# Two TensorE steps of a scan are given a due time in the scheduler that orders the queues

## The chip, the core and the metric

The kernel runs on one core of a Trainium2 chip. The metric is device time in microseconds (us), the median of several runs. Engines are named as in the profile: PE is TensorE's matmul (PEld its weight load), DVE is VectorE, ACT is ScalarE, POOL is GpSimd, SP is SyncE, which only issues transfers here.

## The reference, cut to what matters

Four images of 96 channels and 64 x 64 pixels pass through four layers. Layer 0 is a selective scan in four directions, layer 1 a deformable convolution, layer 2 a Fourier mixer with a quantised feed-forward part, layer 3 linear attention with another feed-forward part. Only the scan of layer 0 is touched:

```python
def step(h, inp):
    d_t, u_t, b_t, c_t = inp
    dA = jnp.exp(d_t[..., None] * A)
    h = dA * h + (d_t * u_t)[..., None] * b_t[:, :, None, :]
    y = jnp.einsum('bkdn,bkn->bkd', h, c_t)
    return (h, y)
h0 = jnp.zeros(u.shape[:3] + (A.shape[-1],), u.dtype)
_, ys = lax.scan(step, h0, (dl, ul, bl, cl))
```

There are 4 images, 4 directions, 192 channels, 16 states for each channel and 4096 positions.

## The kernel before

**Units.** The scan is cut into 1536 units: 4 images x 4 directions x 4 stretches of 1024 positions x 3 groups of 64 channels x 8 sets of 8 channels. A unit has 8 channels times 16 states on the 128 partitions and 1024 positions along the free dimension. Eight units in a row form a block, which ends in one tile of sums, `py`. Each unit passes through these steps:

- `fetch` (L956): a transfer on ACT's queue brings the step widths into `da`, one of six buffers, five units ahead.
- `decay` (L1000): ACT turns `da` into exp(da * A).
- `inflow` (L1006), the **spreading product**: two matmuls copy the unit's 8 rows of delta times u over the 16 states, into `db` in PSUM. `db` has two buffers of 1024 float32 per partition, so the product of unit n+2 writes where the scan of unit n reads.
- `enter` (L1020): DVE multiplies `db` by B in place.
- `recur` (L1028): DVE runs the scan itself, from `da` and `db` into `hh`, one of six buffers.
- `weigh` (L1035, L1037): POOL keeps the last state and multiplies `hh` by C.
- `total` (L1056), the **state sum**: for a pair of units, four matmuls sum the 16 states into `py`. The first pair of a block (`u.i == 0`) opens `py`, in three directions of four with four more matmuls (L1051) that bring in an earlier direction or the skip term. There is one `py` tile, so opening it waits for the copy out of the block before.
- `settle` (L1067): ACT copies a finished `py` to `yb`; `store` (L1074) sends it out from SP's queue.

**The loop over units.** `scan` goes once through its loop for each unit n and emits, in this order, a few loads, `inflow(n+1)`, `decay(n+2)`, for odd n `total(n-5, n-4)`, `fetch(n+5)`, `recur(n)`, `weigh(n-2)` and, at the end of a block, `settle` and `store`. Then it yields, and other work is emitted until none fits: this is called the **fill** below.

**The fill.** Two streams supply it. One (`ends`) prepares the inputs of the scans of images 1 to 3 (convolution L750, `steps` L827 to L880) and then carries each image through layers 2 and 3, one image after another. The other (`middle`) takes the scanned images through the end of layer 0 (`behind`, L1120 to L1177) and through layer 1 (sampling L1369 to L1425). Both are generators; `pipe` runs several chains of steps side by side.

**The clock.** Each engine executes its instructions in the order in which they were emitted; `in_program_order` fixes that order. `Clock` decides it: it keeps for each engine an estimated end, `ends`, to which each emitted step adds its estimated cost. The costs here are 0.8 for a product, 1.22 for `enter`, 2.33 for a scan, 2.55 for `weigh`, 1.5 for a sum and 1.3 more where it opens `py`. A fill step is emitted only where `has_room` finds its inputs ready and its engines no further ahead of `now()` than `AHEAD` (3.0 us for PE, 3.0 DVE, 5.0 ACT, 7.0 POOL). `now()` is the end of DVE's queue or `due`, whichever is later, and `due` moves on by `PACE`, 4.5 us, with each unit. `self.scanned[1]` is the estimated end of the latest scan. One step of the scan is already left to the clock: `precede`, which `pipe` calls ahead of each fill step, emits `enter` of the next unit first when that fill step has DVE work and the product is estimated to be done by then.

A state sum makes itself wait, in the estimate, for three things:

```python
ready = max(u.weighed, v.weighed, self.settled if u.i == 0 else 0.0)
u.summed = v.summed = self.net.clock.add(PE, 1.5 + 1.3 * (u.i == 0), ready)
```

Of the kernel before, what the change touches and what calls it, by code (L numbers as in the profile page):

```python
# [1 line left out]

# [1 line left out]

# [191 lines left out]
PE, DVE, ACT, POOL = range(4)  # L196
# [10 lines left out]
class Clock:  # L207
# [4 lines left out]
    def __init__(self):  # L212
# [8 lines left out]

        self.enter, self.entered = None, 0.0

    def now(self):
        return max(self.ends[DVE], self.due) if self.own is None else self.own

# [15 lines left out]
    def precede(self, work):  # L242


        if self.enter and work[DVE] and self.own is None and self.entered + MARGIN <= self.ends[DVE]:
            self.enter()

    def add(self, engine, us, ready):
        self.ends[engine] = max(self.ends[engine], ready) + us
        return self.ends[engine]  # L250
# [99 lines left out]
class Net:  # L350
# [29 lines left out]
    def load(self, name, pool, tag=None):  # L380
        src = self.ins[name]
        t = pool.tile(list(src.shape), F32, name="w_" + name, tag=tag or "w_" + name)
        self.nc.sync.dma_start(t, src)
        return t
# [158 lines left out]
class Layer0:  # L543
# [340 lines left out]
    def scan(self):  # L884


        units = [
            Unit(b, k, step, g, i, q)
            for b in range(B)
            for k in ((1, 3, 0, 2) if b else (0, 1, 3, 2))  # L890
            for step in range(NT)
            for g in range(NG)
            for i in range(4)
            for q in range(2)
        ]
        ahead = 5
        loaded = 0
        clock = self.net.clock

        def at(m):  # L900
            return units[m] if 0 <= m < len(units) else None

        def made(u):
            return all(
                (u.b, u.k, both, 2 * u.j + h) in self.ready for both in (False, True) for h in range(2)
            )

        for n in range(len(units) + 7):
            for m in range(loaded, min(n + ahead + 1, len(units))):
                while not made(units[m]):  # L910
                    yield False
            if n == 0:
                while loaded < ahead:
                    self.fetch(units[loaded], units[loaded - 1] if loaded else None)
                    loaded += 1
                self.decay(at(0))
                self.decay(at(1))
                self.inflow(at(0))
                self.next = at(0)
                self.enter()  # L920

            for period, tick, load in ((24, 12, self.fetch_step), (8, 2, self.fetch_block)):
                u = at(n - n % period + period)
                if n % period == tick and u is not None and made(u):
                    load(u)
            for stage, m in ((self.inflow, n + 1), (self.decay, n + 2)):
                if at(m) is not None:
                    stage(at(m))
            if n % 2 == 1 and at(n - 5) is not None:
                self.total(at(n - 5), at(n - 4))  # L930
            if loaded < len(units):
                self.fetch(units[loaded], units[loaded - 1])
                loaded += 1
            if at(n) is not None:
                self.recur(at(n), at(n - 6).summed if n >= 6 else 0.0)
            if at(n - 2) is not None:
                self.weigh(at(n - 2))
            if n % 2 == 0 and at(n - 6) is not None and at(n - 6).i == 3:
                self.settle(at(n - 6))
            if n % 2 == 1 and at(n - 7) is not None and at(n - 7).i == 3:  # L940
                self.store(at(n - 7))
            clock.unit(self.scanned[1])
            self.next = at(n + 1)
            if self.next is not None:
                clock.enter, clock.entered = self.enter, self.next.spread
            yield True
            if clock.enter:
                self.enter()
# [913 lines left out]
```

## Time and profile before

| what | us |
|---|---|
| median of 3 runs | 8791.93 |
| lowest and highest | 8787.54, 8800.51 |
| the profiled execution's own time | 8796.72 |
| its span, first to last instruction | 8794.9 |
| scans: first product to last sum | 197 to 7511 of the span |
| after the last scan | 7511 to 8795 |

| engine | busy in the span | busy from 197 to 7511 us |
|---|---|---|
| PE | 6606.4 (75%) | 5441.07 |
| DVE | 6862.6 (78%) | 6252.56 |
| ACT | 4917.9 (56%) | 4427.94 |
| POOL | 5603.0 (64%) | 5224.41 |

The mean granted PE clock is 0.813. How to read it: the scan phase takes five sixths of the span, and the DVE has the most work in it; what follows it is the last image's way through the other layers and what was left over of the image before. The span is one execution, profiled; its own time is 4.8 us above the median.

### The profile page before, as it was taken

How to read it: one execution, taken by the hardware profiler on the slowest of the kernel's cores; microseconds unless marked ns; L12 is line 12 of the kernel's file. 1: busy time of each engine (PE TensorE's matmuls, PEld its weight loads, DVE VectorE, ACT ScalarE, POOL GpSimd, SP SyncE). 2: the span in 40 equal slices, each digit the busy share in tenths (PEclk: the TensorE clock that was granted, in tenths of full speed). 3: DMA queues.
4: the chain of work that ended last, by engine and by line, in shares of the span. 5: the costliest groups of instructions: out<-in, count | busy, mean ns of one | idle time of the engine just before them, and what ended most of it. 6: DMA issues, size and time to landing. Idle time of an engine off the chain costs nothing.

```text
span 8794.9 us, 96335 instructions
## 1 busy us (share of the span) xinstructions
PE 6606.4 (75%) x31960; PEld 2922.3 (33%) x31960; DVE 6862.6 (78%) x5155; ACT 4917.9 (56%) x9030; POOL 5603.0 (64%) x4291
## 2 busy tenths in 40 slices
PE   6665877679677776877677687777768887779697
PEld 2211221123232322321222354322325552367283
DVE  2799989989798988778899887788887878367414
ACT  4554566546577776655666765345676665322323
POOL 0565666666588887656688886566888776167000
PEclk8876887779788777887778788877888887888887
DMA  3577677877788888777788888766888787255110
GB/s 87 165 199 191 180 194 216 213 185 196 197 234 238 234 225 211 188 186 190 213 237 223 233 221 195 184 167 181 217 209 224 210 219 165 62 164 174 28 52 11
DMA packets 775990, 1608.41 MB, mean 183 GB/s; under 512 B 247809, under 2 KB 339357, under 8 KB 773382
## 3 DMA queue, kind: packets, MB, share of 16 engines
q10 hardware_dynamic: 244224, 843.17, 36.9%
q1 hardware_dynamic: 457542, 532.51, 22.4%
q0 software_dynamic: 73728, 226.57, 9.8%
q8 instruction: 257, 4.21, 0.2%
q14 instruction: 239, 1.96, 0.1%
HBM read 1345.62 MB, written 256.29 MB: 182 GB/s over the span
## 4 chain that ended last, share of the span: by engine, by line
PE 34%; DVE 27%; DMA 17%; ACT 8%; issue 7%; POOL 2%; SPq 2%; ACTq 1%; DVEq 0%; POOLq 0%
DVE hh L1028 13%; DVE db L1020 7%; DMA du<-du 4%; PE pc L750 4%; PE py L1056 4%; PE f L1496 3%; PE ps L1402 3%; DMA da<-de 3%; PE db L1006 3%; ACT g L1381 2%; DMA bc<-bcd 2%; PE pd L1418 2%; ACT da L1000 2%; PE h L1537 1%; POOL hh L1037 1%
## 5 line engine op out<-in xcount | busy, mean ns | idle before, releaser
L1037 POOL TENSOR_TENSOR hh<-hh,bc 128x1024 f32<-128x1024 f32 x1536 | 3661.5, 2386 | 385.4 <-DVE hh L1028 275.6
L1028 DVE TENSOR_TENSOR_SCAN hh<-da,st,db 128x1024 f32<-128x1024 f32 x1152 | 2700.8, 2344 | 183.4 <-PE py L1056 63.9
L1020 DVE TENSOR_TENSOR db<-db,bc 128x1024 f32<-128x1024 f32 x1536 | 1862.9, 1213 | 579.5 <-PE db L1006 577.9
L1000 ACT ACTIVATE da<-da,w_al 128x1024 f32<-128x1024 f32 x1536 | 1740.4, 1146 | 628.8 <-DMA da<-de 207.6
L1006 PE MATMUL db<-du,rep 96*128 96x512 bf16 x3072 | 1093.9, 444 | 899.2 <-DVE hh L1028 853.0
L1369 POOL DMA_INDIRECT g<-table,idx x1152 | 1213.2, 1053 | 366.5 <-issue 179.2
L1056 PE MATMUL py<-hh,w_fold 128*32 128x512 f32 x6144 | 1050.0, 757 | 7.5 <-issue 3.7
L1381 ACT ACTIVATE g<-g,wt 128x96 f32<-128x96 f32 x3456 | 963.8, 364 | 157.6 <-DVE hh L1028 52.4
L1028 DVE TENSOR_TENSOR_SCAN hh<-da,db 128x1024 f32<-128x1024 f32 x384 | 877.3, 2285 | 96.9 <-PE py L1056 43.7
L1006 PEld LDWEIGHTS <-rep 96*128 96x128 bf16 x3072 | 281.2, 106 | 1872.0 <-issue 1195.2
L1402 PE MATMUL ps<-w_ident,g 128*96 128x128 f32 x3744 | 694.4, 328 | 195.8 <-ACT g L1381 130.5
L838 POOL TENSOR_TENSOR lw<-lw,w 128x512 f32<-128x512 f32 x192 | 243.9, 1270 | 722.1 <-DVE w L836 651.0
L1402 PEld LDWEIGHTS ps<-w_ident,g 128*96 128x96 f32 x3744 | 495.7, 145 | 570.3 <-ACT g L1381 258.5
L1035 POOL COPY st<-hh 128x1 f32<-128x1 f32 x1152 | 231.4, 201 | 668.7 <-DVE hh L1028 625.0
L750 PE MATMUL pc<-pad,wc 96*128 96x512 f32 x1152 | 570.7, 629 | 12.2 <-DVE rl L840 3.7
L1410 ACT COPY st<-ps 96x384 f32<-96x384 f32 x384 | 179.7, 474 | 457.6 <-PE ps L1402 415.0
L869 PE MATMUL pr<-ex,w_ident 128*128 128x512 f32 x384 | 281.3, 823 | 152.6 <-DVE ex L859 83.8
L750 PEld LDWEIGHTS pc<-pad,wc 96*128 96x128 f32 x1152 | 220.8, 199 | 320.3 <-issue 284.7
L1056 PEld LDWEIGHTS py<-hh,w_fold 128*32 128x32 f32 x6144 | 154.6, 122 | 493.0 <-issue 367.5
L827 PE MATMUL pd<-xd,w_dtw 103*64 103x512 f32 (+1 forms) x512 | 249.1, 740 | 53.6 <-DVE rl L840 28.4
L1418 PE MATMUL pd<-st,wdc 96*128 96x256 f32 x1152 | 286.5, 396 | 3.6 <-ACT st L1410 1.8
L1505 ACT COPY d<-f 128x512 f32<-128x512 f32 x192 | 111.8, 583 | 305.3 <-PE f L1496 291.2
(252 smaller groups left out, 8829.0 us busy)
## 6 DMA issues: line engine op xcount, KB each, us to landing
da<-de ACTq DMA_DIRECT2D x1536, 512.0 KB
du<-du SPq DMA_DIRECT2D x512, 192.0 KB
bc<-bcd SPq DMA_DIRECT2D x128, 512.0 KB
du<-du SPq DMA_DIRECT2D x128, 384.0 KB
y<-yb SPq DMA_DIRECT2D x384, 128.0 KB
de<-rl SPq DMA_DIRECT2D x128, 256.0 KB
m<-in_dft SPq DMA_DIRECT2D x128, 256.0 KB
ad<-y ACTq DMA_DIRECT2D x192, 128.0 KB
```

What stands on the lines that cost most here:

```text
L750: nc.tensor.matmul(pp, lhsT=wc[:, q, g * 128 : (g + 1) * 128], rhs=pad[:, r0 + dy : r0 + dy + NR, dx : dx + W], start=(q == 0), stop=(q == 8),
L869: nc.tensor.matmul(pr, lhsT=net.ident, rhs=ex, start=True, stop=False)
L1000: self.net.nc.scalar.activation(u.da, u.da, AF.Exp, scale=self.al[:, a : a + 1])
L1006: self.net.nc.tensor.matmul(db[:, h, :], lhsT=self.rep[:96, u.s % 4, :], rhs=u.du[u.s // 4][:, h * CH : (h + 1) * CH], start=True, stop=True,)
L1020: self.net.nc.vector.tensor_mul(u.db, u.db, u.bc[:, 0, :])
L1028: nc.vector.tensor_tensor_scan(u.along(u.hh), u.along(u.da), u.along(u.db), first, ALU.mult, ALU.add)
L1037: self.net.nc.gpsimd.tensor_mul(u.hh, u.hh, u.bc[:, 1, :])
L1056: nc.tensor.matmul(py[p0 : p0 + 32], lhsT=self.fold[:, u.i, :], rhs=hc[:, h * CH : (h + 1) * CH], start=u.sums["add"] is None and u.i == 0 ...
L1369: nc.gpsimd.indirect_dma_start(out=g[:, k, :], out_offset=None, in_=self.tables[b % 2], in_offset=bass.IndirectOffsetOnAxis(ap=idx[:, n : ...
L1381: nc.scalar.activation(pixel, pixel, AF.Identity, scale=wt[:, n, c : c + 1])
L1402: nc.tensor.matmul(pt[:, k, :], lhsT=g[:, k, c * C : (c + 1) * C], rhs=net.ident, is_transpose=True, start=(c == 0), stop=(c == corners - 1),)
L1418: nc.tensor.matmul(po, lhsT=wdc[:, k, :], rhs=st[:, k, :], start=(k == 0), stop=(k == 8))
```

## The change

The product of unit n+2 and the sum of a pair are no longer emitted at the head of the next unit only. They are put into a list of the clock, `early`, each with the time from which it is due: the product from the estimated end of scan n, the sum from the estimated end of the later `weigh`. `precede`, which runs ahead of each fill step that `pipe` emits, now also emits every entry of that list that is due by PE's estimated end, if the fill step has PE work. What is still in the list at the next unit's head is emitted there, where both steps stood before.

```diff
@@ class Clock
+        self.early = []
...
         if self.enter and work[DVE] and self.own is None and self.entered + MARGIN <= self.ends[DVE]:
             self.enter()
+        if work[PE] and self.own is None:
+            for due in [e for e in self.early if e[0] <= self.ends[PE]]:
+                self.early.remove(due)
+                due[1]()
...
@@ def scan, head of a unit
-            for stage, m in ((self.inflow, n + 1), (self.decay, n + 2)):
-                if at(m) is not None:
-                    stage(at(m))
-            if n % 2 == 1 and at(n - 5) is not None:
-                self.total(at(n - 5), at(n - 4))
+            while clock.early:
+                clock.early.pop(0)[1]()
+            if n == 0:
+                self.inflow(at(1))
+            if at(n + 2) is not None:
+                self.decay(at(n + 2))
...
@@ def scan, ahead of the yield
+            if at(n + 2) is not None:
+                clock.early.append((self.scanned[1], partial(self.inflow, at(n + 2))))
+            if n % 2 == 0 and at(n - 4) is not None:
+                u, v = at(n - 4), at(n - 3)
+                clock.early.append((max(u.weighed, v.weighed), partial(self.total, u, v)))
             yield True
```

No instruction is added or removed, and no buffer changes. `self.settled`, the third thing that a sum waits for, is not in the due time of the list.

More of the change, by code (lines that the diff above doesn't have):

```diff
@@ L1 @@
 from contextlib import ExitStack
+from functools import partial
 import numpy as np
```

## The prediction

> **What bounds the kernel now.** I read the page's groups first, then busy time by stretch, the waits of DVE and PE, and a timeline of the worst wait.
>
> The groups give the scan's cost on DVE, one product (L1020) and one scan (L1028) for each of 1536 units:
>
> ```profile
> L1028 DVE TENSOR_TENSOR_SCAN hh<-da,st,db 128x1024 f32<-128x1024 f32 x1152 | 2700.8, 2344 | 183.4 <-PE py L1056 63.9
> L1020 DVE TENSOR_TENSOR db<-db,bc 128x1024 f32<-128x1024 f32 x1536 | 1862.9, 1213 | 579.5 <-PE db L1006 577.9
> ...
> L1006 PE MATMUL db<-du,rep 96*128 96x512 bf16 x3072 | 1093.9, 444 | 899.2 <-DVE hh L1028 853.0
> ...
> L1028 DVE TENSOR_TENSOR_SCAN hh<-da,db 128x1024 f32<-128x1024 f32 x384 | 877.3, 2285 | 96.9 <-PE py L1056 43.7
> ```
>
> A unit needs 1.21 + 2.34 = 3.55 us of DVE. Busy time by stretch, cut at the first product and the last sum, shows how far from that the scans are (columns: stretch, length, then busy us of PE, PEld, DVE, ACT, POOL, PE clock, DMA share, GB/s):
>
> ```profile
> 197.00:7511.00 7314.00, 5441.07 (x24486) 2174.39 (x24486) 6252.56 (x4219) 4427.94 (x8110) 5224.41 (x3960) 0.81 0.77 203
> 7511.00:8795.00 1284.00, 1035.79 (x7204) 696.64 (x7202) 577.28 (x875) 391.98 (x793) 369.56 (x316) 0.83 0.29 83
> ```
>
> 7314 / 1536 is 4.76 us a unit. DVE is busy for 6252.6: 5441 for the scan's own two steps and 812 for fill. It idles for 1061. The waits in the same stretch say on what, and what PE waits for in turn:
>
> ```profile
> DVE db L1020 <- PE db L1006: 577.9, 209, 31.2
> DVE hh L1028 <- PE py L1056: 107.6, 77, 17.7
> DVE w L836 <- ACT w L833: 43.3, 32, 7.3
> ...
> PE db L1006 <- DVE hh L1028: 853.0, 449, 15.9
> ```
>
> So 686 of 1061 idle us end with exactly the two steps that the change moves. DVE is the bound of this phase, but through the order of PE's queue, not through PE's capacity: PE idles for 7314 - 5441 = 1873 us, 853 of them at a product whose `db` buffer a scan still holds. The worst case, in the timeline:
>
> ```profile
> 5489.02 2.35 DVE L1028 TENSOR_TENSOR_SCAN hh<-da,st,db 128x1024 f32<-128x1024 f32 x1
> ...
> 5505.77 2.07 PE L1125 MATMUL pc<-ya,w_cen_a 128*128 128x512 f32 x2 [18.74 <-POOL ya L1120]
> ...
> 5513.00 0.83 PE L1006 MATMUL db<-du,rep 96*128 96x512 bf16 x2
> ...
> 5513.87 1.23 DVE L1020 TENSOR_TENSOR db<-db,bc 128x1024 f32<-128x1024 f32 x1 [22.49 <-PE db L1006]
> ```
>
> The product at 5513 could have run from 5487, when its buffer came free. It stands behind a fill matmul that waits 18.74 us for late data.
>
> The phase after the scans ends with the stream that takes images through layers 2 and 3 in turn: in the trace image 1 leaves at 7716, image 2 at 8309 and image 3 at 8787, while the sampling of image 3 is over at 8172. Fill that does not fit beside the scans therefore comes back at the end.
>
> **What the Trainium skill says.** "PSUM — Partial Sum Buffer", section Engine vs sequencer instructions, says that matmuls start and complete in program order and that the other three engines' queues are strict FIFO. The trace agrees: nothing passed L1125 for 18.74 us. So a moved step holds up all that is queued behind it. The same page, Specifications, gives 8 banks of 2 KiB (512 float32) per partition: `db` takes four, `py` one, the fill three, so the one-unit reach of `db` and the single `py` stay the limits. The trace shows both: products wait for scans, opening a sum waits for `yb`. "Perfetto Trace Analysis", Identifying the Most-Contended Engine, takes occupancy as a fair measure for VectorE and warns that it isn't for TensorE; I use PE's busy time only to split it into fill and scan.
>
> **The change, part by part.** It adds and removes no instruction. A moved product is two weight loads and two matmuls (0.6 us), a moved sum eight records of each (1.07 us), twice that where it opens `py` with L1051. Neither issues a transfer, and only PE's queue changes directly. The call itself costs nothing on the chip.
>
> *Where they go.* Read unit by unit from the trace, the product of n+2 starts 2.37 us after the end of scan n on average, over 2 us in 643 units of 1534 and over 3 us in 439. Meanwhile PE is busy for 2901 of these 3640 us. In those stretches PE's estimate runs ahead of the scan's, the entry is due at the first or second PE step of the fill, and the product jumps a unit's fill. Where PE is early, it stays where it was.
>
> *Gain at the product.* A product that is earlier by one place can let DVE run on by one unit at most, 3.55 us: the product after it is still behind the same fill. If every late product stood right behind the one before it, the waits would shrink by 540 us; each capped at 3.55 this is 356. About half the late ones should get it, since some entries come due only after the step that blocks, and part of the time saved only moves to the next wait: 0.5 x 356 = 178.
>
> *Gain at the sum.* The sum has been ready for long: it starts 11.5 us (median) after POOL's last product for it. It goes ahead of the fill as well, `hh` comes free sooner, and half of the 107.6 us goes: 54. Together 232.
>
> *Loss at `py`.* The first sum of each block, 192 of them, is due by `weigh` alone, but needs the copy `yb` (ACT, L1067), which was emitted just before in the same unit. It used to stand one unit later. The copy ends 2.31 us (median) after the product that would now stand ahead of it; counted from the end of scan n plus 0.6 us for the product, it is late by 251 us summed over the blocks. For that long PE stands still with fill, and sometimes the next product, behind it; the clock charges it too, so less fill is emitted. PE is 74% busy in the scans, so 251 x 0.74 = 186 us of PE work is lost to them. It returns at the end, where PE is busy for 1035.8 of 1284 us (81%): 186 / 0.81 = 230. The scans lose DVE fill in return: 812 us of it goes with about 3090 us of PE fill (5441 less 1094, 1050 and about 205 for L1051, whose first 768 of 1152 records take 136.7), 0.26, so 48 come off. Loss 182. Bounds: 0 if PE has nothing to do just then; 562 us of holding (copy against product, all blocks), so 0.74 / 0.81 x 562 less 108 = 405, if PE is always short.
>
> *Loss at the fill.* PE's fill of a unit now starts behind a product that waits for a scan, up to a unit later. DVE consumers stand in fixed places: of the 64 `d<-h` (L1545) within the scans a quarter started less than 1.4 us after their matmul, half less than 2.8. Some 400 DVE fill steps read PE's results directly; a quarter of them late by 1 us is 100. That is an estimate; the trace of before has no such order. Bounds: 0, as `enter` now comes ahead of DVE's fill and gives 1.21 us of cover, and 300.
>
> *At nothing:* `decay`, `fetch`, `weigh`, `recur` and the loads keep their order on ACT, POOL, DVE and SP. `enter` ahead of fill moves 1.21 us, it adds none; its cover is the product's earlier place.
>
> Sum against the profiled execution's 8796.7: -232 + 182 + 100 = +50, so 8847. That execution is 4.8 above the median of the runs: **8842**. What is late next: fill results on DVE, and the opening of `py`.
>
> **Rivals.**
> - *Faster (0.36).* The hold at `py` falls into PE's idle time, of which there are 1873 us. Then three quarters of the gains, 0.75 x (356 + 108) = 348, stand against 200 of losses: about 8645, from 8560 to 8770. For it: DVE waited little for fill before (43.3 us is the largest). Against: each wait taken from DVE makes PE the one that waits. It decides if the hold costs under 80 us.
> - *No difference (0.10).* The entries are seldom due, and are emitted at the unit's head as before: 8792. The 643 late products speak against it.
> - *Much slower (0.12, part of slower).* PE loses its reserve: the 1087 products that did not wait for a scan now wait 0.25 us each, 270 us with fill behind. By the conversion above this is 195 more: about 9035. The 853 us, 449 waits, speak for it; PE's 26% of slack against.
> - *The forecast (0.42):* 8800 to 8930 on its own.
>
> Below 0.2% (18 us) this kernel's measurement can't tell a change from none. **Chances:** faster 0.36, same 0.10, slower 0.54. The range runs from 8610 (a tenth below, in the faster case) to 8980 (a tenth above).
>
> **What would show it.** Right: L1020's wait for L1006 falls from 578 to about 400, L1056's hold on scans to 55; PE's wait for `yb` at L1051 (105 us in 36 cases) grows past 250; PE's wait for scans at L1006 rises above 853; the last sum comes before 7511 and the end phase is longer than 1284. Wrong: an end phase no longer than before with the scans shorter (the faster rival), DVE's new waits at L840, L836 and L1545 above 300 us (much slower), or a PE order that hardly differs.

## The result, and the profile after

| | before | after |
|---|---|---|
| median of the runs, us | 8789.74 (4 runs, 8776.73 to 8800.51) | 9018.36 (4 runs, 9008.85 to 9027.76) |
| ratio, 95% interval | | **1.0266** (1.0246 to 1.0285): slower |
| the profiled execution, span, mean granted PE clock | 8796.72, 8794.9, 0.813 | 9026.73, 9024.9, 0.816 |

Slower by 2.7%, 230 us between the spans. The direction was forecast, the size was not: 50 us, and a range that ended at 8980.

The groups of the changed kernel; the product is now L1019, `enter` L1033, the scan L1041, the opening matmuls of `py` L1064, the sum L1069, the copy to `yb` L1080, `decay` L1013:

```profile
L1041 DVE TENSOR_TENSOR_SCAN hh<-da,st,db 128x1024 f32<-128x1024 f32 x1152 | 2700.1, 2344 | 320.0 <-PE py L1069 150.3
L1033 DVE TENSOR_TENSOR db<-db,bc 128x1024 f32<-128x1024 f32 x1536 | 1857.4, 1209 | 312.5 <-PE db L1019 311.4
...
L1019 PE MATMUL db<-du,rep 96*128 96x512 bf16 x3072 | 1109.9, 450 | 1045.6 <-DVE hh L1041 966.0
...
L1041 DVE TENSOR_TENSOR_SCAN hh<-da,db 128x1024 f32<-128x1024 f32 x384 | 876.8, 2283 | 139.6 <-PE py L1069 71.6
```

Counts are those of before and durations nearly so; what has moved is the idle time before the steps. `enter` waits 312.5 instead of 579.5: the early product works. The two kinds of scan wait 459.6 (320.0 + 139.6) instead of 280.3, and about half of that (221.9) is on the sum L1069. Busy time by stretch, cut at the first product and the last sum (columns as in the prediction):

```profile
195.00:7426.00 7231.00, 5240.65 (x21996) 1992.33 (x21996) 6201.56 (x4155) 4308.82 (x7896) 5197.57 (x3927) 0.80 0.77 203
7426.00:9025.00 1599.00, 1290.20 (x9698) 888.30 (x9694) 645.19 (x987) 492.10 (x975) 409.88 (x333) 0.86 0.28 78
```

The scans are 83 us shorter and what follows them is 315 us longer. Some 2,490 matmuls (24486 less 21996) have left the scans, and as many have come to the end. Of the 83 us, 51 are work of DVE that has left (6252.56 to 6201.56) and 32 are idle time: 7231 - 6202 = 1029, against 1061. **The shorter scans have nearly the same idle time in them.** Not every instruction stays where it was: 48 quantising steps of the fill run on DVE now, 32 of which were on ACT and 16 on POOL. The kernel writes them so when they come after the scans. e7 below has the same 48 and the time of before, so the loss isn't theirs. The waits of DVE, over the whole span (us in total, times, longest):

```profile
DVE db L1033 <- PE db L1019: 311.4, 107, 31.4
DVE hh L1041 <- PE py L1069: 221.9, 94, 13.3
...
DVE hh L1041 <- ACT da L1013: 72.7, 58, 8.8
```

The product's wait fell by 267 us (from 577.9). The sum's rose from 107.6 by 114, the one for `decay` from 21.6 by 51. Added up over all steps of DVE in the scans, `enter` idles 267 us less, the scan steps 179 more and the fill's steps 75 more (212 to 287), and the 20 us for which DVE of before idled between its last scan and the last sum are gone. That makes the 32, but for rounding. The waits of PE:

```profile
PE db L1019 <- DVE hh L1041: 966.0, 594, 17.1
PE py L1064 <- ACT yb L1080: 262.0, 90, 13.5
...
PE py L1069 <- ACT yb L1080: 25.7, 16, 7.2
```

PE's wait for the copy of the block before, 105.1 in 36 cases, is now 262.0 + 25.7 in 106. One such case in the timeline of the changed kernel (start, us, engine, line, operation; in brackets the idle time before it and what ended it):

```profile
2591.21 0.59 PE L1019 MATMUL db<-du,rep 96*128 96x512 bf16 x2 [0.82 <-DMA da<-de]
...
2594.61 1.21 DVE L1033 TENSOR_TENSOR db<-db,bc 128x1024 f32<-128x1024 f32 x1
2595.48 1.28 ACT L410 ACT_TABLE_LOAD   x1
...
2596.77 1.15 ACT L1013 ACTIVATE da<-da,w_al 128x1024 f32<-128x1024 f32 x1
...
2597.95 0.59 ACT L1080 COPY yb<-py 128x512 f32<-128x512 f32 x1
...
2598.58 1.93 PE L1064 MATMUL py<-ad,w_ident 128*32 128x512 f32 x8 [6.78 <-ACT yb L1080]
...
2600.29 1.93 PE L1069 MATMUL py<-hh,w_fold 128*32 128x512 f32 x8
...
2602.16 1.03 PE L1019 MATMUL db<-du,rep 96*128 96x512 bf16 x2
...
2602.42 2.29 DVE L1041 TENSOR_TENSOR_SCAN hh<-da,db 128x1024 f32<-128x1024 f32 x1 [6.60 <-PE py L1069]
```

PE reaches the opening of `py` right behind an early product, at 2591.8, and stands there for 6.78 us: ACT still has fill and a `decay` ahead of the copy. The next product and all fill stand behind it. The scan at 2602.42 is unit 502. With six `hh` buffers it writes where unit 496 wrote, and 496 = 8 x 62 is the first unit of a block, whose sum is the one that opens `py`. So it waits 6.60 us for that sum. This is the general place: adding the idle time (gaps over 0.15 us) ahead of the scans of units 6, 14, 22 and so on, the ones that need the opening sum's buffer, gives 214 us in after and 95 in before; each of the other seven places in the block has 2 to 38 in after. Of the 214, 183 end with the sum, and 141 of these follow an opening that had just waited for the copy.

The Trainium skill, "Perfetto Trace Analysis", section Optimization Strategy, says that the same gap repeating on the engine that should be saturated can mean too little memory, too few buffers for instance, for the next tile. The trace agrees on where, at every eighth scan; no run here had a second `py`, and e7 below takes the wait away without one.

### The profile page after: what moved, and what is told of

Same layout as the page of the kernel before. It is cut to its first block, busy times and chain, and to the rows that moved or that the text cites. A ratio compares the mean times of both kernels' runs of the same rounds, so it can differ in the third digit from the quotient of the medians.

```text
span 9024.9 us, 96146 instructions
## 1 busy us (share of the span) xinstructions
PE 6655.5 (74%) x31960; PEld 2929.8 (32%) x31960; DVE 6879.6 (76%) x5203; ACT 4898.6 (54%) x8998; POOL 5616.5 (62%) x4275
## 4 chain that ended last, share of the span: by engine, by line
PE 30%; DVE 29%; DMA 15%; ACT 9%; issue 9%; POOL 5%; SPq 1%; ACTq 1%; DVEq 0%; POOLq 0%
DVE hh L1041 15%; DVE db L1033 7%; DMA du<-du 4%; PE f L1509 3%; POOL hh L1050 3%; PE py L1069 3%; PE ps L1415 3%; PE pc L757 3%; PE db L1019 2%; DMA da<-de 2%; ACT g L1394 2%; PE pd L1431 2%; ACT da L1013 2%; PE py L1064 1%; PE h L1550 1%
## 5 line engine op out<-in xcount | busy, mean ns | idle before, releaser
L1041 DVE TENSOR_TENSOR_SCAN hh<-da,st,db 128x1024 f32<-128x1024 f32 x1152 | 2700.1, 2344 | 320.0 <-PE py L1069 150.3
L1033 DVE TENSOR_TENSOR db<-db,bc 128x1024 f32<-128x1024 f32 x1536 | 1857.4, 1209 | 312.5 <-PE db L1019 311.4
L1013 ACT ACTIVATE da<-da,w_al 128x1024 f32<-128x1024 f32 x1536 | 1736.6, 1145 | 518.4 <-DMA da<-de 206.3
L1019 PE MATMUL db<-du,rep 96*128 96x512 bf16 x3072 | 1109.9, 450 | 1045.6 <-DVE hh L1041 966.0
L1382 POOL DMA_INDIRECT g<-table,idx x1152 | 1238.8, 1075 | 377.1 <-issue 171.6
L1069 PE MATMUL py<-hh,w_fold 128*32 128x512 f32 x6144 | 1065.7, 759 | 78.2 <-ACT yb L1080 25.7
L1019 PEld LDWEIGHTS <-rep 96*128 96x128 bf16 x3072 | 268.8, 107 | 2205.7 <-DVE hh L1041 1071.6
L1041 DVE TENSOR_TENSOR_SCAN hh<-da,db 128x1024 f32<-128x1024 f32 x384 | 876.8, 2283 | 139.6 <-PE py L1069 71.6
L1415 PE MATMUL ps<-w_ident,g 128*96 128x128 f32 x3744 | 717.2, 332 | 242.1 <-ACT g L1394 139.8
L1069 PEld LDWEIGHTS py<-hh,w_fold 128*32 128x32 f32 x6144 | 159.2, 123 | 602.5 <-issue 401.7
L1596 DVE TENSOR_TENSOR t<-t,o 96x512 f32<-96x512 f32 x64 | 81.0, 1269 | 342.3 <-PE o L1594 342.3
```

The lines of the kernel that those rows point to most:

```text
L1013: self.net.nc.scalar.activation(u.da, u.da, AF.Exp, scale=self.al[:, a : a + 1])
L1019: self.net.nc.tensor.matmul(db[:, h, :], lhsT=self.rep[:96, u.s % 4, :], rhs=u.du[u.s // 4][:, h * CH : (h + 1) * CH], start=True, stop=True,)
L1033: self.net.nc.vector.tensor_mul(u.db, u.db, u.bc[:, 0, :])
L1041: nc.vector.tensor_tensor_scan(u.along(u.hh), u.along(u.da), u.along(u.db), first, ALU.mult, ALU.add)
L1069: nc.tensor.matmul(py[p0 : p0 + 32], lhsT=self.fold[:, u.i, :], rhs=hc[:, h * CH : (h + 1) * CH], start=u.sums["add"] is None and u.i == 0 ...
L1382: nc.gpsimd.indirect_dma_start(out=g[:, k, :], out_offset=None, in_=self.tables[b % 2], in_offset=bass.IndirectOffsetOnAxis(ap=idx[:, n : ...
```

## The experiments

Three terms are used in all of them, read from the records. *Scans* and *end* are the two stretches above. *Fill* is PE's busy time in the scans less the time in which a product or a sum runs (L1064 counts as sum). *Waits* are DVE's, for the product, for the sum (`hh`) and for `decay`. All but the ratio are microseconds of one profiled execution.

The theories before the first ones ran: **T1**, the early opening of `py` waits for the copy and costs PE its fill; **T1a**, it does so through the scheduler's `Clock`, which charges that wait to PE as if PE worked and so emits less fill; **T1b**, it does so on the chip, PE really standing. **T2**, the rival: the early product takes PE's reserve, since PE now stands at products that wait for scans.

The runs of a group (e1 to e4, e5 to e8, e9 to e12, e13 to e15) shared a chip with runs of before. Before took 8865.49 on the first group's chip and 8762 to 8790 on the others'. So the microseconds of e1 to e4 carry some 80 of the chip's own, which stages they are in is not known, and across groups only ratios compare closely.

Of the ranges set down beforehand, those of e5, e6 and e10 were met, and those of T1 for the times of e2 and e7. e1, e3, e4, e11 and e12 fell between the theories, e9 took signs from both, and e8, e13, e14 and e15 came out as neither theory allowed.

| kernel | ratio (95%) | scans | end | fill | waits: product / sum / decay | PE at `py` for `yb` |
|---|---|---|---|---|---|---|
| before | 1 | 7314 | 1283 | 3175 | 578 / 108 / 22 | 105 |
| after | 1.0266 (1.0246 to 1.0285) | 7231 | 1599 | 2914 | 311 / 222 / 73 | 262 |
| e1 product only | 1.0094 (1.0057 to 1.0131) | 7250 | 1495 | 3030 | 222 / 347 / 70 | 111 |
| e2 sum only | 1.0221 (1.0181 to 1.0261) | 7218 | 1647 | 2928 | 635 / 61 / 17 | 224 |
| e3 opening at the head | 1.0120 (1.0081 to 1.0160) | 7289 | 1496 | 3083 | 202 / 366 / 68 | 122 |
| e4 no charge | 1.0125 (1.0085 to 1.0166) | 7316 | 1467 | 3061 | 341 / 214 / 108 | 229 |
| e5 none due | 1.0016 (0.9997 to 1.0036) | 7297 | 1285 | 3167 | 558 / 107 / 22 | 106 |
| e6 before, charge | 1.0098 (1.0072 to 1.0124) | 7178 | 1482 | 3024 | 478 / 93 / 42 | 95 |
| e7 after, copy early | 0.9992 (0.9978 to 1.0005) | 7241 | 1343 | 3128 | 289 / 130 / 158 | 0 |
| e8 before, copy early | 1.0086 (1.0060 to 1.0111) | 7404 | 1276 | 3247 | 705 / 57 / 49 | 0 |
| e9 sum only, no charge | 1.0162 (1.0136 to 1.0188) | 7415 | 1303 | 3171 | 731 / 31 / 29 | 158 |
| e10 e7 with a charge | 1.0085 (1.0057 to 1.0114) | 7101 | 1596 | 2930 | 270 / 83 / 121 | 23 |
| e11 product and copy early | 1.0060 (1.0036 to 1.0084) | 7336 | 1317 | 3211 | 205 / 421 / 72 | 0 |
| e12 copy in the due time | 1.0172 (1.0151 to 1.0193) | 7300 | 1441 | 3031 | 263 / 347 / 79 | 153 |
| e13 e7, decay early | 1.0121 (1.0100 to 1.0142) | 7291 | 1356 | 3195 | 400 / 137 / 21 | 4 |
| e14 e13, no charge | 1.0040 (1.0025 to 1.0055) | 7334 | 1260 | 3218 | 358 / 172 / 36 | 2 |
| e15 before, decay early | 1.0127 (1.0112 to 1.0142) | 7426 | 1280 | 3203 | 672 / 137 / 5 | 119 |

### One half of the change at a time: e1, e2

In e1 the sums are never due, in e2 the products, so these stay at the unit's head (the lines of the diffs from here on are cut or broken to fit):

```diff
e1
-                clock.early.append((max(u.weighed, v.weighed), partial(self.total, u, v)))
+                clock.early.append((float("inf"), partial(self.total, u, v)))
e2
-                clock.early.append((self.scanned[1], partial(self.inflow, at(n + 2))))
+                clock.early.append((float("inf"), partial(self.inflow, at(n + 2))))
```

> The changed kernel with only the product of unit n+2 in the clock's list; the sums are emitted at the unit's head as before. Two theories share the blame for 1599 us after the last sum (1284 before). T1: the first sum of a block, queued one unit earlier, waits for the copy of py, and that wait costs PE fill. Then without early sums most of the damage is gone: end phase about 1340, scans about 7400 from first product to last sum less some 150 us of db waits, in all 8700 to 8820. T2: the early product takes PE's reserve, so PE stands at products waiting for scans and fill is pushed out. Then the end phase stays near 1550 and the time near 8980.

> The changed kernel with only the sums in the clock's list; products are emitted at the unit's head as before. T1 (the opening sum waits for the copy of py): end phase 1550 to 1600, and without the product's gain the scans are as long as before or longer, so 8980 to 9080. T2 (the product takes PE's reserve): close to before, 8790 to 8830, PE's wait for the copy grown but covered by PE's idle time.

The sum alone (1.0221) costs most of the loss, and it has the long end phase: 1647. That is T1's side. But the product alone isn't free (1.0094). The waits of DVE in e1:

```profile
DVE hh L1041 <- PE py L1069: 346.7, 175, 7.4
...
DVE db L1033 <- PE db L1019: 221.7, 56, 32.0
...
DVE hh L1041 <- ACT da L1013: 70.4, 38, 7.3
```

The product's wait falls by 356 and the sum's rises by 239: a sum that stays at the head is now late for a DVE that gets on faster. **A wait taken away at `db` comes back at the next ring, `hh`.**

### The opening alone: e3, e12

e3 leaves only the opening sum of each block at the head; e12 lets it be due, but not before the copy is estimated to be done:

```diff
e3
+                due = float("inf") if u.i == 0 else max(u.weighed, v.weighed)
+                clock.early.append((due, partial(self.total, u, v)))
e12
+                due = max(u.weighed, v.weighed, self.settled if u.i == 0 else 0.0)
+                clock.early.append((due, partial(self.total, u, v)))
```

> The changed kernel, but the 192 sums that open py stay at the unit's head; products and the other 576 sums are in the list. T1: PE's wait for the copy at the opening sum returns to about 105 us, the end phase to 1300 to 1380, the time to 8720 to 8850. T2: no change from the changed kernel, 8980 to 9020.

> The changed kernel with the end of the copy added to the due time of the sums that open py, so that one is queued early only when PE's estimate has passed the copy. T1a: between the changed kernel (1.0266) and the one with opening sums at the head (1.012), as it leaves fewer waits in the estimate: 1.005 to 1.016. T1b: PE's wait for the copy on the chip decides: if it stays over 200 us, over 1.018.

With the opening back at the head e3 has no more wait for `yb` than before had (122 against 105), and the ratio falls from 1.0266 to 1.0120: about half of the loss hangs on where that one sum in four stands. It doesn't fall to 1, since `hh` is now late: 366 on the sum, and the idle time at the eighth-unit places, whatever ended it, is 370 against 214 in after, so the opening sum is the late one. e12 has the same signs, 347 on the sum and 302 at these places, and is worse. So neither placing of the opening mended the order: early, it waits for the copy and holds PE; late, the scan six units on waits for it.

### Is it the charge or the standing: e4, e5, e6, e9

e4 and e9 take the copy out of the estimate (e9 on top of e2), so that PE's wait stays and is not charged. e6 does the reverse on the kernel before: it charges each opening 1.55 us more, 192 x 1.55 = 298 us, and adds no wait on the chip. e5 is the changed code with nothing ever due.

```diff
e4, e9
-        ready = max(u.weighed, v.weighed, self.settled if u.i == 0 else 0.0)
+        ready = max(u.weighed, v.weighed)
e6, on before
-        u.summed = v.summed = self.net.clock.add(PE, 1.5 + 1.3 * (u.i == 0), ready)
+        u.summed = v.summed = self.net.clock.add(PE, 1.5 + (1.3 + 1.55) * (u.i == 0), ready)
```

> The changed kernel with every due time kept; only the clock's estimate of a sum leaves the copy of py out of what it waits for, so the estimate no longer sets PE's time back at the opening sum. The chip still waits for the copy. T1a: the damage comes from the estimate, which finds less room for fill: end phase falls to 1300 to 1400 and the time to 8750 to 8880 although PE's wait at the opening sum stays at 262 us or more. T1b: the damage is PE standing still on the chip: fill is emitted but runs late, the scans get longer than 7350 and the time stays above 8980.

> A control: the changed kernel's list with due times that never come, so both steps are emitted at the unit's head. Both theories: the order of before and its time within 0.3%; the profile gives the phases of before on the chip of the other runs of this call.

> The kernel before, where only the clock's estimate of the sum that opens py is 1.55 us longer (192 times, 298 us in all). No step is moved by a due time and none waits for anything new on the chip. T1a (time that the clock charges to PE is fill that isn't emitted): PE fill in the scans falls by 100 to 250 us, the end phase grows by 120 to 300, the time by 0.8 to 2.2%. T1b (only the real waits of PE count): within 0.3% of before.

> The kernel with only the sums in the list, where the clock's estimate of a sum leaves out the copy of py; its counterpart with the copy in the estimate took 1.0221 of before. On the chip PE still waits some 220 us for the copy. T1a (the estimate costs the fill): PE fill in the scans back within 60 us of before, end phase under 1400, time 0.995 to 1.008. T1b (PE standing still costs it): end phase or scans stay long, 1.015 to 1.025.

e5 is before's time (1.0016, interval across 1), so the list itself costs nothing. Its stretches, then those of e6:

```profile
195.00:7492.00 7297.00, 5438.42 (x24487) 2176.65 (x24488) 6258.17 (x4219) 4428.96 (x8110) 5224.17 (x3960) 0.81 0.78 203
7492.00:8776.40 1284.40, 1028.26 (x7202) 689.07 (x7200) 577.35 (x875) 392.85 (x793) 373.81 (x316) 0.84 0.29 83
```

```profile
195.00:7373.00 7178.00, 5304.51 (x23408) 2099.28 (x23406) 6213.87 (x4192) 4349.32 (x7966) 5189.62 (x3939) 0.82 0.78 206
7373.00:8855.50 1482.50, 1175.04 (x8282) 786.48 (x8280) 617.93 (x950) 452.80 (x905) 386.92 (x321) 0.84 0.28 78
```

With no wait added, the charge alone, at a size chosen for the run, moves 1,080 matmuls out of the scans, makes them 119 us shorter and the end 198 longer, and costs 1%. That is T1a, and it gives the **exchange rate**: 143 us of fill less (3167 to 3024) is 0.83 us of scans gained and 1.38 of end lost for each, 0.55 net. In the changed kernel e4 brings back 147 us of fill and 1.4%. Its chip makes the microseconds uncertain; in matmuls, 24050 run within the scans, so 2,054 of the 2,490 that had left are back, and still the kernel is 1.25% slower than before.

e9 shows the other part. It has before's fill (3171 against 3175) and almost before's end (1303), and is still slower by 1.6%: its scans take 7415, 100 more. Its waits on DVE and on PE:

```profile
DVE db L1033 <- PE db L1019: 731.2, 284, 30.7
```

```profile
PE py L1064 <- ACT yb L1080: 158.0, 64, 9.5
```

PE stands 158 us for `yb`, and products behind it are late: DVE waits 731 for them, 153 more than in before. A longer wait for products alone would not show the cause, since e8 below has one without any wait for `yb`. But the trace of e9 shows it: 147 us of the 731, in 41 cases, fall on a product that is the next in PE's queue after an opening that waited for the copy; in before it is 25 us in 13 cases. So 122 of the 153 stand behind that wait, and this is T1b. Both ways of T1 act, and neither is all of it.

### Taking the wait away: e7, e8, e10, e11

PE's wait for `yb` can go, with the dependence kept, if the copy is emitted earlier: right after the last sum of its block, up to two units ahead of where it stood. Nothing else in the program's text moves.

```diff
e7
@@ def scan
-            if n % 2 == 0 and at(n - 6) is not None and at(n - 6).i == 3:
-                self.settle(at(n - 6))
@@ def total, at its end
+        if u.i == 3:
+            self.settle(u)
```

e8 is the same edit on before, e10 is e7 with e6's charge, e11 is e7 with e1's sums at the head.

> The changed kernel, with the copy of py emitted right behind the sum that closes it and no longer up to two units later, so that the next opening sum finds it done. T1 (the opening sum's wait for the copy is the damage): PE's wait for the copy falls from 262 to under 80 us, DVE's waits for hh fall from 222 to under 100, db waits stay near 300, the end phase falls from 1599 to 1300 to 1420 and the time to 0.985 to 1.005 of before. T2 (the product ahead of the fill takes PE's reserve): DVE's waits shift to other places, the time stays over 1.01 of before.

> The kernel before with the same earlier copy and nothing else. PE's wait for the copy is 105 us there and DVE's wait at every eighth scan 95 us, so both theories allow 0.985 to 1.003 of before. It tells how much of the run beside it is owed to the copy alone.

> The kernel with the copy of py right behind the closing sum, which was level with before, where the clock's estimate of an opening sum is made 1.55 us longer. Nothing on the chip waits more. T1a: PE fill in the scans falls by 150 to 300 us, end phase grows from 1343 to 1500 or more, time 1.008 to 1.022. T1b: level with before, 0.995 to 1.005.

> Product in the list, sums at the unit's head, copy of py right behind the closing sum. T1: the product alone took 1.0094, with DVE's waits for hh at every eighth scan (192 of 460 us); with the copy early these fall below 100 and the time to 0.99 to 1.003. T2 (the product takes PE's reserve, whatever the sums do): it stays at 1.007 to 1.012.

**e7 takes back the whole 2.7%**: 0.9992, over 20 runs of it and 31 of before. Its stretches and its waits on DVE (`enter` is L1031 here, the scan L1039):

```profile
197.00:7438.00 7241.00, 5385.85 (x24381) 2182.03 (x24380) 6204.21 (x4200) 4381.50 (x8026) 5213.13 (x3943) 0.81 0.78 205
7438.00:8781.00 1343.00, 1073.45 (x7308) 707.41 (x7307) 615.06 (x942) 419.71 (x847) 379.42 (x317) 0.84 0.28 80
```

```profile
DVE db L1031 <- PE db L1017: 289.4, 88, 30.6
...
DVE hh L1039 <- ACT da L1011: 157.8, 103, 8.8
...
DVE hh L1039 <- PE py L1067: 129.7, 71, 10.9
```

The scans are as short as in after (7241), with 214 us more fill in them, and the end is 256 shorter. The copy now ends 3.6 us (median) ahead of the end of the scan of the next block's fifth unit, where it ended 2.08 after it in the changed kernel and 0.37 after it in before; the eighth-unit places are back at 91. But it's no gain on before: the wait for `decay` has grown to 158. And a wait has changed sides. The copy now stands in ACT's queue ahead of its input, and ACT waits for the closing sum, in e7 and then in e8:

```profile
ACT yb L1080 <- PE py L1067: 231.8, 98, 9.7
```

```profile
ACT yb L1067 <- PE py L1054: 222.3, 91, 20.7
```

In after this wait is 4.0 us, in before 8.7. PE's 262 us have become 232 of ACT, an engine with more idle time.

It isn't that the early copy is good in itself: in before it costs 0.9% (e8). There sums and products stay late, and DVE waits 705 for products, 127 more than in before. The waits for a product ahead of which PE's longest stand was for ACT grew from 224 to 332 us, so most of the growth stands behind ACT; that the copy's wait on ACT is what made ACT late is likely and was not tested. So the parts don't add, and "the copy explains 2.7%" holds only of the changed order. **With the late copy the change costs 2.7%; with the early copy it gains 1.0%** (8772.49 against e8's 8858.41), which only makes good what the early copy had cost.

e10 puts the charge back, nearly without PE's wait (23 us):

```profile
195.00:7296.00 7101.00, 5229.90 (x22504) 2030.87 (x22504) 6202.67 (x4148) 4318.45 (x7914) 5187.39 (x3923) 0.80 0.78 207
7296.00:8892.00 1596.00, 1284.73 (x9188) 859.33 (x9184) 652.64 (x994) 482.53 (x957) 409.59 (x337) 0.85 0.28 78
```

The end is after's, 1596 against 1599, but the scans are 130 us shorter than after's. Fill 198 less, scans 140 less, end 252 more: 0.71 and 1.27, net 0.57, the same rate as from e6. Against after's 9018 this gives a size for what PE's standing costs: at the same fill (2930 and 2914) the scans of after are 130 us longer. The shares depend on the order in which the parts are taken off: the charge is worth 1.4% in the changed kernel (e4) and 0.9% once the copy is early (e10 against e7).

e11 gives the product its due once the copy is early: 1.0060, with 421 us on the sum. Its counterpart is e8 (1.0086), which has the early copy and no early product, and the intervals of the two overlap. So with the early copy the early product without early sums costs nothing that these runs can tell, which leaves little for T2; early sums win 0.7% more (e7). e1's lost fill (3030) is there again in e11 (3211), so that loss too went through the copy.

### The next wait in turn: e13, e14, e15

In e7 the wait on `decay` is what has grown. e13 emits `decay` three units ahead instead of two, e14 does so without the charge, e15 does it on before.

```diff
e13, e14 (e15 alike, in before's list of stages)
-            if at(n + 2) is not None:
-                self.decay(at(n + 2))
+            if at(n + 3) is not None:
+                self.decay(at(n + 3))
```

> The kernel with the copy of py right behind the closing sum, and the decay of a unit emitted three units ahead of its scan and no longer two. There DVE's wait for products had halved (289 us) but its waits at the scan for da had grown from 22 to 158. If that wait is what eats the product's gain, it falls under 60 us, the scans get 60 to 140 us shorter and the time is 0.984 to 0.995 of before. If DVE's slack is fixed elsewhere (fill that PE gets late), the wait moves again, to hh or db, and the time stays at 0.996 to 1.003.

> The same, with the copy of py left out of the clock's estimate of a sum. The estimate has little left to lose there, so the charge theory allows no more than 0.3% against the run beside it; if the chip's waits at the opening sum return because more fill is emitted, it is slower by 0.3 to 1%.

> The kernel before with the decay three units ahead and nothing else. DVE waited 22 us for da there, so both theories: 0.997 to 1.003 of before.

e13 and e14 are slower than e7, and e15 is slower than before. The wait for `decay` goes (158 to 21), but ACT now reaches `decay` before its transfer has landed. The waits on ACT, then on DVE, in e13:

```profile
ACT da L1012 <- DMA da<-de: 884.3, 406, 10.4
```

```profile
DVE db L1032 <- PE db L1018: 399.6, 145, 30.8
...
DVE hh L1040 <- PE py L1068: 136.6, 94, 10.4
```

It was 211.0 us in e7. ACT stands, and the fill's work on ACT stands behind it: PE's waits for ACT grow from 507 to 644 us, and DVE's wait for the product goes up again from 289 to 400. With six `da` buffers and this order of the loop the fetch can't come a unit earlier, since its buffer is the one that the scan of unit n is about to read. e14 is 0.8% faster than e13, where the charge theory allowed 0.3%: the end is 96 us shorter without the charge (1260 against 1356). So the estimate still charges for the copy when it comes early, and e7 without that charge was not run. Nor was a seventh `hh` buffer, which would relieve the sum. No version beat the kernel before; e7 equals it.

## Why the prediction was right and where it was wrong

**Right: the direction and the signs of the mechanism.** The opening of `py` waits for `yb` beyond 250 us (251 worked out, 262.0 measured); PE waits for scans longer (966.0, from 853.0); the last sum comes earlier (7426) and the end is longer (1599, from 1284); the product's wait falls. The step "fill that does not fit comes back at the end" carried the result: the end's 315 us are more than the whole loss.

**Luck in the direction.** The sign of the +50 hung on the estimate of 100 for DVE's late fill. What that term stood for, DVE's fill steps waiting for PE, rose by 39 us (17 to 56). With 39 in its place the sum is -11. The direction came right because the gain failed.

**By stage.** The forecast has the scans 180 us shorter (232 of waits and 48 of DVE's fill less, 100 more at the fill) and the end 230 longer. Measured are 83 (32 idle, 51 of DVE's work) and 315. So the prediction missed by about 100 us in the waits of the scans and by 85 at the end; the 48 was right.

**Wrong, first: the gain of 232 in the waits, which was to shorten the scans.** At the product 178 was forecast and 267 taken away. At the sum 54 was to go and 114 was added: I counted the sum as ready for long, which is so of its inputs, while the opening one needs `py` and stands longer for it, with the sixth scan after it behind. And hardly any of the gain became time: DVE's idle time in the scans went from 1061 to 1029 only. What left `db` came up at `hh`, at `da` and at the fill's steps. "Part of the time saved only moves to the next wait" was in the working, as a reason for one half; it was nearly the whole.

**Wrong, second: two terms of the loss at `py`.** Fill lost: 251 x 0.74 = 186 forecast, 253 to 261 measured (3167 and 3175, less 2914). The wait in all was right, but 107 us of it were there in before, so 181 are new (288 less 107, the sum's 25.7 and 1.6 included), and 251 was put down as if all were. At 0.74 these 181 are 134 us of fill; about twice that was lost. That the clock charges the wait too was said and given no term. e4 brings 147 us of fill back without the charge. Then the rate: I took 1.23 us of end for each us of fill and 0.26 back in the scans, 0.98 net. e6 and e10 show 1.27 to 1.38 and 0.71 to 0.83, 0.55 to 0.57 net. The scans get more back than DVE's own fill work, since less fill on PE also lets the products come sooner: in e6 DVE's wait for them is 478, against 558 in e5. Two readings were off without touching the 251. L1020, called a product where the groups are read, is `enter`. And the 2.31 us and the bound of 562 were read against the product of unit n+1, while the opening stands behind that of n+2, and the copy of before ends 1.84 us (median) ahead of that one.

**The sum, remade from the runs.** This is a check that the parts fit, with rates taken from two other orders. Against e5, whose order is before's: fill is 253 less, so by the rates the end should be 321 to 349 longer and the scans 180 to 210 shorter. The end is 315 longer, which fits within 6. The scans are only 66 shorter, so by difference 114 to 144 were lost in them, to PE standing at `py` and to the waits that moved; e10 puts that at 130 in another way. Net, 315 - 66 = 249, which is the difference of the two spans (9024.9 less 8776.4). How the 130 divide between the late opening and the early product wasn't settled.

**The loss of 100 at the fill's DVE steps** was too large: 39 us for PE's results, as said, and 75 for whatever these steps waited for.

**The rivals.** Faster: its condition, a hold at `py` under 80 us, failed with 262; and e7, where PE has no such hold, took the time of before, not some 8645. No difference: 107 waits instead of 209 at the product say that the entries were often due. Much slower: its time, 9035, is near the measured one, but not by its mechanism. It asked for 270 us more of PE waiting at products; there were 113. The early product alone costs 0.9% in e1, with the sums late for it, and nothing that can be told once the copy is early (e11 against e8).

## What to carry to other kernels

Before you count a wait on the bound engine as gained, name the next buffer ring on the same path and ask whether it comes free any sooner: here 267 us left `db`, 165 reappeared at `hh` and `da` and 75 at the fill, and idle time fell by 32. A step that is queued early must have all that it waits for early too; where one accumulator tile is reused, look at its copy first, since here that alone took the changed kernel from 1.0266 to 0.9992. Then see which engine waits instead: on the order of before the same move cost 0.9%. In an order fixed by estimates, a wait that is charged as work displaces other work, and what it costs is found where that work comes back, not at the wait.

## What the runs showed of the hardware

PE's wait was passed on almost whole to another engine: 6.78 us at `py` became 6.60 us of DVE's idle time at the scan that needed the sum behind it. What the Trainium skill, "PSUM — Partial Sum Buffer", section Engine vs sequencer instructions, states of this order is borne out by the timeline of unit 502. The Trainium skill, "Perfetto Trace Analysis", section Matmuls, advises that independent groups rotate through PSUM banks so that the copy of one overlaps the next group's matmuls; e7, where the overlap comes from an earlier copy and not from a second bank, bears out the aim (wait for `yb` 262 to nothing), and no run here had a second bank. The wait did not vanish from the chip: ACT stood 231.8 us in its place.

Not expected: how closely a queue follows its transfers. Moving `decay` by one unit of some 4.8 us took ACT's wait for the landing of `da` from 211.0 us (e7) to 884.3 in 406 cases (e13), and on the order of before from 207.6 to 997.3 (e15).
